# Ten rows of unused matmuls behind the last batch of a four-layer graph attention kernel

## The chip, the cores and the metric

The kernel runs on one core of one Trainium2 chip. The metric is the device time of an execution in microseconds (us), from many engines working side by side: PE (TensorE, with its weight loads counted apart as PEld), DVE (VectorE), ACT (ScalarE), POOL (GpSimd) and SP (SyncE, which issues most DMAs). The time before is 2933.31 us, the median of two runs (2930.95 and 2935.68 us).

## The reference

32 graphs of 512 nodes with 256 features each go through four attention layers, all in fp32. What is computed for one layer, cut to its core:

```python
h = jnp.maximum(_layernorm(x), 0.0)
Wh = h @ W
e = leaky_relu(Wh @ a1 [:, :, None] + Wh @ a2 [:, None, :], alpha)
e = jnp.where(adj, e, -inf)
x = x + act(softmax(e) @ Wh)      # elu, relu, elu with 4 heads
```

The fourth layer is an MLP (256 to 512), an attention without a mask over 512 features, a second MLP (512 to 256) and an attention with the mask; then relu, and the sum with x. The result is x after the fourth layer.

## The kernel before, in words

The function `fast` keeps the weights, the adjacency (`maskT`, bf16, 128 partitions by 4 by 512) and the identity in SBUF for the whole run. Its logits are exponentials of sums, so that a masked weight tile is one DVE instruction (L353, max and multiply with `maskT`). One batch is a generator that yields between pieces of work. Four such streams run at a time (`NS` is 4), each working through every fourth batch, and the loop at the end of `fast` always advances the stream whose due time is the earliest. [...] The last batch, number 31, has nothing beside it at its end: its pieces at L676 to L720 follow one another, with one row tile per step (`n = 1`).

Nearly all matmuls are fp32 and are issued at L66 (`matmul`) and L70 (`transpose`). In the trace an fp32 matmul leaves two records on PE, each with a weight load of its own on PEld, and a transpose leaves one. A matmul writes to a bank of PSUM (128 partitions by 512 fp32), handed out by `bank()` at L76 to L80: four names with two buffers each, used in turn when no other stream is active, so that a bank comes back after eight allocations.

Behind the loop, L789 to L799 make a single number, `flag`: the DVE reduces what `note` (L306) has collected in `seen` to `bad` (128 by 1), PE transposes `bad` to one row (L797), and the DVE reduces this to `one` (L798) and compares (L799). All engines then load `flag` (L1203) and branch on it (L1204). In this run it is zero, and the engines jump over the second version of the kernel, `general`, to the end of the program.

Of the kernel before, what the change touches and what calls it, by code (L numbers as in the profile page):

```python
# [19 lines left out]
FP = mybir.dt.float32  # L20
# [4 lines left out]
OP = mybir.AluOpType  # L25
AX = mybir.AxisListType

EPS = 1.0e-5
P = 128
# [6 lines left out]
def fast(ctx, tc, flag, x, adj, w0, a0, w1, a1, w2, a2, mlp1_w, mlp1_b, mlp2_w, mlp2_b,  # L36
         w_fc, a_fc, w_hand, a_hand, out):
    nc = tc.nc
# [13 lines left out]
    work = ctx.enter_context(tc.tile_pool(name="work", bufs=2))  # L52
# [24 lines left out]
    def bank():  # L77

        own = [turn[0], *(i for i in range(NS) if i not in active and i != turn[0])]
        banks[0] += 1  # L80
        return psum.tile([P, N], FP, tag=f"b{own[banks[0] % len(own)]}", name="b", bufs=8 // NS)
# [3 lines left out]
    ident = const.tile([P, P], FP, name="ident")  # L85
# [78 lines left out]
    for h in range(NH):  # L164
        t, r = divmod(h * D, P)
# [6 lines left out]
    WM1 = const.tile([P, KF, H], FP, name="WM1")  # L172
# [24 lines left out]
    maskT = const.tile([P, NT, N], BF, name="maskT")  # L197
# [572 lines left out]
    while ready:  # L770
        i = min(ready, key=ready.get)
# [14 lines left out]
            ready[i] = wait  # L786


    worst = const.tile([P, 3], FP, name="worst")  # L789
    nc.vector.tensor_reduce(worst[:, 0:1], seen, AX.X, OP.max)  # L790
    nc.vector.tensor_scalar(worst[:, 0:1], worst[:, 0:1], LIMIT, None, op0=OP.is_gt)
# [3 lines left out]
    p = bank()  # L795
    transpose(p[:1, :P], bad, ident)
    one = const.tile([1, 1], FP, name="one")  # L797
    nc.vector.tensor_reduce(one, p[:1, :P], AX.X, OP.max)  # L798
    nc.vector.tensor_scalar(flag, one, 0.5, None, op0=OP.is_gt)  # L799


@with_exitstack
# [394 lines left out]
@with_exitstack  # L1197
def kernel(ctx: ExitStack, tc: tile.TileContext, *args):
    nc = tc.nc
    keep = ctx.enter_context(tc.tile_pool(name="keep", bufs=1))  # L1200
    flag = keep.tile([1, 1], I32, name="flag")
    fast(tc, flag, *args)
    bad = nc.values_load(flag[0:1, 0:1], min_val=0, max_val=1)  # L1203
    with tc.If(bad > 0):  # L1204
        general(tc, *args)
# [27 lines left out]
```

## Time and profile before

| what | us |
|---|---|
| median of two runs | 2933.31 |
| span of the profiled execution, first to last instruction | 2929.6 |
| PE busy in the span | 2858.9 (98%) |
| DVE busy | 2219.9 (76%) |
| ACT busy | 1536.8 (52%) |
| last matmul for the result (transpose of `rT`) starts | 2920.99 |
| transpose of `bad` starts | 2921.10 |
| `flag` is written | 2922.26 |
| last counted instruction (sum into x, L715) ends | 2925.34 |
| mean TensorE clock granted, as a share of full speed | 0.996 |

The profiled execution is the only one with a trace. Its span leaves out what an execution does before the first and after the last instruction; the median of the runs is 3.7 us above it. Engines in a trace have a row each, and a row shows when an instruction was busy and what it waited for. Register, branch, semaphore and load-to-register instructions are not counted as busy: they are in the trace's records, but in none of the groups. So between 2925.34 us and the end at 2929.64 us the groups show nothing, though the program is still at work: the last DMAs of the output land, and the engines load the flag, branch and meet at a barrier.

### The profile page before, as it was taken

The numbers are of one execution on the slowest core, as the hardware profiler recorded it, in microseconds if no ns is written. First come the engines' busy times: TensorE is split into PE (matmuls) and PEld (weight loads), VectorE is DVE, ScalarE is ACT, GpSimd is POOL, SyncE is SP. The second block draws the span as 40 slices with busy tenths as digits, with TensorE's granted clock in tenths as the row PEclk, the third lists the DMA queues.
The fourth block names the chain that finished last, engine by engine and source line by source line (L and its number), as shares of the span: only waits on it lengthen the run. The fifth ranks groups of instructions, "written<-read, shape, count | busy, mean of one in ns | idle before, by whom it ended". The sixth has DMA issues, their size and how long they took to land.

```text
span 2929.6 us, 43083 instructions
## 1 busy us (share of the span) xinstructions
PE 2858.9 (98%) x15177; PEld 2329.5 (80%) x15177; DVE 2219.9 (76%) x5676; ACT 1536.8 (52%) x3922; POOL 502.3 (17%) x515
## 2 busy tenths in 40 slices
PE   8999999999999999999999999999999999999998
PEld 6777887877888877888877888788887788877876
DVE  4677877778778778778778777787787787777764
ACT  4444455555555555555554556545555555555444
POOL 0011112112122111122021121111221111211220
PEclk9999999999999999999999999999999999999999
DMA  3033223233223333233332233222332322323230
GB/s 94 19 102 102 80 88 116 91 98 95 88 94 106 93 100 98 84 102 96 100 102 80 89 115 93 91 97 91 94 116 80 102 93 88 104 93 96 90 107 30
DMA packets 193182, 270.89 MB, mean 92 GB/s; under 512 B 17024, under 2 KB 156094, under 8 KB 192960
## 3 DMA queue, kind: packets, MB, share of 16 engines
q1 hardware_dynamic: 163200, 169.76, 18.5%
q0 software_dynamic: 29760, 98.30, 10.4%
q8 instruction: 123, 2.02, 0.3%
q14 instruction: 99, 0.81, 0.1%
HBM read 152.62 MB, written 115.39 MB: 91 GB/s over the span
## 4 chain that ended last, share of the span: by engine, by line
PE 82%; DVE 10%; ACT 4%; DMA 3%; issue 1%; SPq 0%; POOL 0%; DVEq 0%; POOLq 0%; ACTq 0%
PE b L66 75%; PE b L70 7%; DVE st L269 2%; DMA g<-table,at 2%; DVE sums L641 1%; DVE xn L280 1%; DVE x L406 1%; DVE y L405 1%; ACT v L325 1%; DVE sums L632 1%; ACT y L505 1%; ACT q L504 1%; DVE w L353 1%; ACT hT L290 1%; DVE tot L646 0%
## 5 line engine op out<-in xcount | busy, mean ns | idle before, releaser
L66 PE MATMUL b<-v,w 128*128 128x65 f32 (+1 forms) x7232 | 1218.0, 321 | 10.6 <-DVE w L353 10.5
L66 PEld LDWEIGHTS b<-v,w 128*128 128x128 f32 x7232 | 1050.0, 191 | 168.7 <-issue 56.1
L66 PE MATMUL b<-WFC,oT 128*128 128x256 f32 (+1 forms) x2048 | 495.2, 380 | 0.0
L66 PEld LDWEIGHTS b<-WFC,oT 128*128 128x128 f32 x2048 | 374.5, 189 | 49.3
L66 PE MATMUL b<-W,hT 128*128 128x259 f32 (+1 forms) x1536 | 388.8, 391 | 22.8 <-DVE v L463 14.1
L353 DVE SCALAR_TENSOR_TENSOR w<-b,v,maskT 128x512 f32<-128x512 f32 x512 | 369.4, 744 | 5.1 <-PE b L70 4.1
L607 POOL DMA_INDIRECT order<-v,at x248 | 277.0, 1117 | 490.7 <-DVE oT L730 152.3
L66 PEld LDWEIGHTS b<-W,hT 128*128 128x128 f32 x1536 | 285.3, 192 | 75.3 <-DVE v L463 17.1
L715 POOL TENSOR_TENSOR x<-x,y 128x512 f32<-128x512 f32 x62 | 87.8, 1416 | 1063.7 <-ACT y L713 950.0
L353 DVE SCALAR_TENSOR_TENSOR w<-spread,v,maskT 128x512 f32<-128x512 f32 x384 | 269.5, 742 | 0.0
L66 PE MATMUL b<-hT,WM 128*128 128x512 f32 x512 | 250.0, 599 | 0.7 <-ACT hT L290 0.7
L66 PE MATMUL b<-oT,WM 128*128 128x512 f32 x512 | 231.2, 594 | 0.0
L655 POOL DMA_INDIRECT g<-table,at x124 | 120.9, 975 | 642.8 <-ACT y L675 292.0
L387 DVE RECIPROCAL rden<-b 128x1 f32<-128x1 f32 (+1 forms) x516 | 77.3, 162 | 184.8 <-PE b L66 183.0
L529 ACT ACTIVATE v<-b,ends 128x256 f32<-128x256 f32 x256 | 118.8, 467 | 177.2 <-PE b L66 172.9
L269 DVE BATCH_NORM_STATS2 st<-x 128x6 f32<-128x256 f32 x512 | 193.3, 409 | 6.4 <-DMA x<-in_x_dram 4.1
L412 DVE TENSOR_TENSOR y<-q,y 128x512 f32<-128x512 f32 (+1 forms) x194 | 132.9, 685 | 82.9 <-ACT q L411 45.0
L339 ACT ACTIVATE oT<-b,bias 128x512 f32<-128x512 f32 x128 | 87.7, 686 | 182.7 <-PE b L66 182.0
L290 ACT ACTIVATE hT<-b 128x512 f32<-128x512 f32 x256 | 146.5, 592 | 70.3 <-PE b L70 70.2
L66 PEld LDWEIGHTS b<-oT,WM 128*128 128x128 f32 x512 | 97.5, 191 | 95.7 <-issue 92.4
L70 PE MATMUL b<-ident,xn 128*128 128x128 f32 x1024 | 147.4, 275 | 6.7 <-DVE xn L280 4.0
L70 PEld LDWEIGHTS b<-ident,xn 128*128 128x128 f32 x1024 | 123.7, 143 | 31.9 <-DVE xn L280 5.2
(143 smaller groups left out, 3748.1 us busy)
## 6 DMA issues: line engine op xcount, KB each, us to landing
table<-sums SPq DMA_DIRECT2D x62, 1032.0 KB
sums<-order SPq DMA_DIRECT2D x62, 516.0 KB
spread<-row SPq DMA_DIRECT2D x96, 256.0 KB
x<-in_x_dram SPq DMA_DIRECT2D x32, 512.0 KB
out_dram<-x SPq DMA_DIRECT2D x62, 256.0 KB
sums<-order SPq DMA_DIRECT2D x62, 129.0 KB
order<-v,at POOLq DMA_INDIRECT x248
g<-table,at POOLq DMA_INDIRECT x124
```

Of the source, the lines that this page charges most:

```text
L66: nc.tensor.matmul(p, w, x, **flags)
L70: instruction = nc.tensor.transpose(p, x, i)
L269: nc.vector.bn_stats(st[:, i, :], xt[:, t0 + i, :])
L290: nc.scalar.activation(hT[:, :, t0 * P:(t0 + 2) * P], p.rearrange("p (k n) -> p k n", k=KF), AF.Relu)
L339: nc.scalar.activation(o[:, f, :], p, AF.Relu, bias=bias[:, f:f + 1])
L353: w = nc.vector.scalar_tensor_tensor(wt[:, j, :], r, t_col(j), maskT[:, j, :], op0=OP.max, op1=OP.mult)
L387: nc.vector.reciprocal(r, den)
L412: nc.vector.tensor_tensor(r, q, r, op=OP.add)
L529: nc.scalar.activation(halves[c][:, t, :F], ps[:, :F], AF.Copy, scale=ends[:, t, 0:1])
L607: nc.gpsimd.indirect_dma_start(out=orders[c], out_offset=bass.IndirectOffsetOnAxis(ap=at[:, 0, t:t + 1], axis=0), in_=halves[c][:, t, :], ...
L655: nc.gpsimd.indirect_dma_start(out=g, out_offset=None, in_=table, in_offset=bass.IndirectOffsetOnAxis(ap=at[:, 1, t:t + 1], axis=0),)
L715: (nc.gpsimd if n == 2 else nc.vector).tensor_tensor(xr, xr, y, op=OP.add)
```

## The change

A function `rows` is called once, behind the loop over the streams and ahead of the reduction of `seen`. It copies 128 by 512 of the weights `WM1` to a tile `half` of type fp32r (DVE), copies the identity to a tile of fp32r that nothing reads, and then issues ten rows of matmuls, each matmul with `start` and `stop` set. A row goes to one bank (the tenth to two), and when it is done a DVE reduction over 64 columns writes one number to `got`, which nothing reads. `keep_in_program_order` ties the matmuls of a row to the order in which they are written. In `tile_position=(r, c)` r is the first row of the array that the matmul uses and c the first column.

```diff
+    rows(nc, tc, work, bank, ident, maskT, WM1)
+
     worst = const.tile([P, 3], FP, name="worst")
...
+FR = mybir.dt.float32r
...
+def rows(nc, tc, work, bank, ident, maskT, WM1):
+    near = WM1[:, 0, :]
+    half = work.tile([P, 512], FR, tag="spread", name="half", bufs=2)
+    nc.vector.tensor_copy(half, near)
+    tile_r = work.tile([P, P], FR, tag="junk", name="tile_r", bufs=1)
+    nc.vector.tensor_copy(tile_r, ident)
+    got = work.tile([P, 16], FP, tag="tot", name="got", bufs=1)
+    sets = []
+
+    def row(count, one):
+        p = bank()
+        for i in range(count):
+            tc.keep_in_program_order(one(p, i))
+        sets.append(p)
+        c = len(sets) - 1
+        nc.vector.tensor_reduce(got[:1, c:c + 1], p[:1, :64], AX.X, OP.max)
+
+    def mm(p, w, x, **at):
+        return nc.tensor.matmul(p, w, x, start=True, stop=True, **at)
+
+    def w_of(t, i):
+        return t[:, i % 4 * P:(i % 4 + 1) * P]
+
+    row(24, lambda p, i: mm(p[:, :65], w_of(maskT[:, 0, :], i), maskT[:, 1, :65]))
+    row(12, lambda p, i: mm(p[:, :195], w_of(maskT[:, 0, :], i), maskT[:, 1, :195]))
+    row(24, lambda p, i: mm(p[:, :66], w_of(half, i), half[:, :66]))
+    row(12, lambda p, i: mm(p[:, :256], w_of(half, i), half[:, :256]))
+    row(12, lambda p, i: mm(p[:, :128], w_of(near, i), near[:, :128]))
+    row(4, lambda p, i: mm(p[:64, :], near[:, i * 64:(i + 1) * 64], near, tile_position=(0, 0)))
+    row(16, lambda p, i: mm(
+        p[i % 2 * 64:i % 2 * 64 + 64, :], near[:, i % 8 * 64:(i % 8 + 1) * 64], near, tile_position=(0, i % 2 * 64)
+    ))
+    row(16, lambda p, i: mm(
+        p[i % 4 * 32:i % 4 * 32 + 32, :], near[:, i * 32:(i + 1) * 32], near, tile_position=(0, i % 4 * 32)
+    ))
+    row(16, lambda p, i: mm(
+        p[i % 4 * 32:i % 4 * 32 + 1, :], near[:, i * 32:i * 32 + 1], near, tile_position=(0, i % 4 * 32)
+    ))
+    q = [bank(), bank()]
+    for i in range(16):
+        r = i % 2 * 64
+        tc.keep_in_program_order(mm(
+            q[i % 2][:, :65], near[r:r + 64, i % 4 * P:(i % 4 + 1) * P], near[r:r + 64, :65],
+            tile_position=(r, 0),
+        ))
+    for i in range(2):
+        nc.vector.tensor_reduce(got[:, 14 + i:15 + i], q[i][:, :64], AX.X, OP.max)
```

In the built program PE's list has the rows behind the last transposes of `rT` for the result and ahead of the transpose of `bad`. The two copies stand on the DVE in layer 2 of the last batch, between weight tiles of its last head (L353), the reductions of rows 1 and 2 among the last elementwise work of the result, and the others behind it. The lists of ACT, POOL and SP keep their work in its order, but for the load of `flag`, which on SP now stands behind the last output DMA and not between two of them.

## The prediction

> **What bounds the kernel now.** I read the page first, for which engine sets the pace, then the groups kept apart by form, for the price of a matmul, then the timeline and the chain of waits over the last 25 us, because the change stands there alone. The page:
>
> ```profile
> PE 2858.9 (98%) x15177; PEld 2329.5 (80%) x15177; DVE 2219.9 (76%) x5676; ACT 1536.8 (52%) x3922; POOL 502.3 (17%) x515
> ```
>
> PE is full for the whole span, and no other engine is. Work added to PE is paid in full unless it falls where PE is idle. The table of windows (PE, PEld, DVE, ACT and POOL busy, granted clock, DMA share, GB/s) shows the one such place:
>
> ```profile
> 2900.00:2921.00 21.00, 20.71 (x87) 14.69 (x86) 8.35 (x24) 10.41 (x25) 2.53 (x2) 1.00 0.08 26
> 2921.00:2929.60 8.60, 0.37 (x4) 0.08 (x2) 3.68 (x12) 3.25 (x9) 0.00 (x0) 0.76 0.21 70
> ```
>
> PE is done at 2921.4 us, and 8.2 us follow without it. The timeline says where PE's list ends, and what a matmul costs there:
>
> ```profile
> 2816.99 3.68 PE L66 MATMUL b<-v,w 128*128 128x65 f32 x32
> 2904.94 3.60 PE L66 MATMUL b<-oT,WM 128*128 128x512 f32 x8
> ...
> 2920.88 0.38 PE L70 MATMUL b<-ident,rT 128*128 128x128 f32 x2
> 2921.10 0.27 PE L70 MATMUL b<-ident,bad 128*1 128x128 f32 x1
> ```
>
> Start to start is a line's length less one record, over the others: (3.60 - 0.59) / 7 = 0.429 us for 512 columns, (3.68 - 0.275) / 31 = 0.110 us for 65; the single records of the second lie 0.1117 us apart, which I use. One fp32 matmul is two records. 0.429 us is 0.84 ns per column, 65 columns would stream in 0.055 us, so 0.112 us must be the load of the 128 columns of weights. The chain of waits ends with
>
> ```profile
> 2924.47 0.43 ACT y L713
> 2924.90 0.02 issue
> 2924.92 0.42 DVE x L715
> ```
>
> that is, with the last elementwise work of the result; the output DMA issued behind it, the branch and the barrier fill the 4.3 us to 2929.64.
>
> [...]
>
> **The change part by part.** Nothing is removed. PE executes in order and the rows stand between the last `rT` transposes and `bad`, so they start at 2921.1, where `bad` started. Row 1 takes the bank of the first average, eight allocations back, which ACT left at 2917.8; later rows find theirs read by 2924 to 2926, while they come at 2927 and later, so I charge no wait for banks.
>
> 1. 24 bf16, 65 columns: half of the fp32 load, 0.060 us: 1.4 us. Bounds 0.030 (streaming 27 ns and a little) and 0.112 [...]: 0.7 to 2.7.
> 2. 12 bf16, 195 columns: half of an fp32 record's 0.84 ns per column, [...] 195 x 0.42 = 82 ns and 2 of overhead: 0.084 us, 1.0 together (1.3 if the load is 0.112).
> 3. 24 fp32r, 66 columns. [...] As one record with the load of an fp32 record: 24 x 0.112 = 2.7 us. Bounds: 1.4 as bf16, 5.4 as full fp32.
> 4. 12 fp32r, 256 columns: in one pass 256 x 0.42 ns and 2 are 0.109 us: 1.3 us; as fp32 the row of `WFC,oT` gives two records 0.216 us apart: 5.2. I take 1.3.
> 5. 12 fp32, 128 columns: 24 records x 0.112 = 2.7 us.
> 6. 4 fp32, 512 columns, one column group: 8 x 0.429 = 3.4 us.
> 7. to 9. Each 16 fp32 matmuls, 512 columns, in two, four and four column groups. Without overlap 32 x 0.429 = 13.7 us each, 41.2 together. With free overlap 6.9 + 3.4 + 3.4 = 13.7. I take a value between: the two records of a matmul use the same group, so the second waits for the first; in program order the next matmul's first record can only run beside this one's second. That is one record time per matmul however many groups there are: 17 x 0.429 = 7.3 us each, 21.9 together.
> 10. 16 fp32, 65 columns, two row groups: the load of 128 columns binds, 32 x 0.112 = 3.6 us; 1.8 if two loads go side by side.
>
> Four changes of mode (into row 6, between 7 and 8, into and out of 10) at the part of a record that normally overlaps, 0.592 - 0.429 = 0.16 us: 0.7 us. Sum S = 1.4 + 1.0 + 2.7 + 1.3 + 2.7 + 3.4 + 21.9 + 3.6 + 0.7 = 38.7 us.
>
> Behind the rows `flag` becomes the last thing in the program. The final matmul drains 0.16; the two reductions over 128 partitions take 0.2 each (0.195 for `seen` 128x48), `one` 0.27, `flag` 0.14, with about 0.06 of hand-over. In the trace's uncounted records, PE loads the flag 0.04 us after it is written (2922.26), is at its branch at 2923.06 and only goes on at 2926.92: 4.66 us from flag to PE past the branch. This was hidden under the last output; now it is on the path. From the last engine past its branch (DVE, 2928.555) to the end took 1.09. So the end is 2921.1 + S + 0.16 + 0.4 + 0.27 + 0.14 + 0.06 + 4.66 + 1.09 = 2966.6, that is S - 1.8 = +36.9 us on 2929.6. The median of the runs stood 3.7 above the span and I leave that: 2933.3 + 36.9 = 2970.2.
>
> The rest I cost at nothing. The copies (0.43 for 128x512, from `W<-raw` at L231, and some 0.2) push the last weight tile of head 3 from 2809.8 to 2810.4; PE reads it at 2816.99, and the DVE idles 3.19 us at 2810.5. Without that cover they would cost 0.6. The reductions of rows 1 and 2 wait for PE at 2922.7 and 2923.7, and L412, L712 and L715 of the result are queued behind them: the last sum into x comes some 0.9 us later, its DMA with it, all under the rows, which run to 2959. SP's later flag load is behind its last DMA, and waits for the flag anyway.
>
> **Rivals.**
> A, my forecast, pairs overlap: +36.9. With the bounds of rows 1 to 4 and 10, 2966 to 2978.
> B, the column groups of fp32 do not overlap at all: S grows by 41.2 - 21.9 = 19.3, +56.2, 2989.6. For: nothing before shows any overlap. [...] This is the case on the other side of 2%: the limit is 58.7 us, so it decides as soon as rows 1 to 4 cost 2.5 us more than I took; with fp32r at the fp32 price (+6.6) it gives 2996.
> C, full packing: S falls by 8.2, +28.7, 2962; with the low ends of rows 1, 3 and 10, 2958. [...]
> D, the clock: the last window was granted 0.76, when PE sat idle. Should partly used columns count as idle and the clock fall to half, S doubles: +75.6, 3009. Against: the table has 1.00 where PE is busy.
> E, the unused rows are dropped, or PE takes them in earlier gaps: 2933, no slower. PE's list holds them all at the end, and PE had no gap of that size; almost excluded.
>
> **How the numbers follow.** A 0.45, B 0.26 (0.09 of it over 2%), C 0.22, D 0.04, E 0.03. About 2% is what a measurement of this kernel tells from no change. Slower by over 2%: 0.09 + 0.04 = 0.13. Faster by over 2% needs an accident: 0.01. The rest, 0.86, is within 2%, though A, B and C are all real additions. The range runs from the low end of C, 2958, to B with part of its upper bound, 2993; outside are E, the lower tip of C, D and the dear half of B, about 0.18. A's own range is 2965 to 2979.
>
> **What would show it.** Rows 7, 8 and 9 last 7.3 us each (A), 13.7 (B), or 6.9, 3.4 and 3.4 (C). Row 6 is 3.4 and row 5 2.7, or the fp32 price is wrong. One record per fp32r matmul, 0.11 us apart in rows 3 and 4. PE's first new matmul at 2921.1, `flag` about 0.9 us after PE's last row, the end 5.8 after that. The granted clock stays at 1.00. It is wrong if the groups behave unlike each other, if the branch is served faster from a flag that comes late, or if fp32r costs like fp32.

## The result, and the profile after

The changed kernel took 2965.9 us, the median of two runs (2965.75 and 2966.06), against 2933.31: a ratio of 1.0111, 95% interval 1.0092 to 1.0131. That is within 2%, inside the range, and 4.3 us below the forecast. A repetition further down puts the ratio at 1.0095, and the traces show what stretched the profiled execution of this first comparison. The page of the changed kernel says

```profile
PE 2893.4 (98%) x15409; PEld 2350.2 (79%) x15409; DVE 2223.4 (75%) x5689; ACT 1536.9 (52%) x3922; POOL 505.4 (17%) x515
```

PE is 34.5 us busier, and its weight loads 20.7. Of the 34.5 us, the rows are 28.0; where the others come from is asked further down. The windows (PE, PEld, DVE, ACT and POOL busy, granted clock, DMA share, GB/s), cut at the start of the rows and at their end, place it:

```profile
2900.00:2929.20 29.20, 28.91 (x130) 21.71 (x129) 13.24 (x34) 15.13 (x35) 2.54 (x2) 1.00 0.06 19
2929.20:2957.60 28.40, 28.37 (x236) 15.97 (x234) 5.20 (x21) 3.24 (x9) 0.00 (x0) 1.00 0.06 20
2957.60:2964.30 6.70, 0.00 (x0) 0.00 (x0) 0.48 (x4) 0.00 (x0) 0.00 (x0) 0.59 0.04 10
```

The rows fill 28.0 us without a gap at a full clock, and 6.7 us of flag, branch and barrier follow. The chain of waits now ends with PE, not with the sum into x:

```profile
2929.44 27.98 PE b L826 x232
2957.42 0.34 DVE got L854 x2
2957.76 0.20 DVE one L800
2957.95 0.02 issue
2957.98 0.14 DVE flag L801
```

The groups kept apart by form (busy us, mean ns of one record) give the rows' share. Row 6 and row 7 have one form, 40 records:

```profile
L826 PE MATMUL b<-WM 128*64 128x512 f32 x40 | 10.5, 595 | 0.0
L826 PE MATMUL b<-WM 128*32 128x512 f32 x32 | 3.6, 595 | 0.0
L826 PE MATMUL b<-WM 128*1 128x512 f32 x32 | 3.6, 592 | 0.0
...
L826 PE MATMUL b<-WM 64*128 64x65 f32 x32 | 2.0, 275 | 0.0
...
L826 PE MATMUL b<-maskT 128*128 128x65 bf16 x24 | 0.9, 193 | 0.0
```

32 records of 512 columns in 3.6 us: if one record of few columns of weights takes 0.429 us like a full one, they ran four at a time. (That it does is shown below, with all of them in one column group.) The weight loads show it too. A line of the timeline is a burst, and from row 7 to row 9 the bursts hold more:

```profile
2940.12 0.14 PEld L826 LDWEIGHTS b<-WM 128*64 128x64 f32 x1 [0.29 <-issue]
2940.55 0.19 PEld L826 LDWEIGHTS b<-WM 128*64 128x64 f32 x3 [0.29 <-issue]
...
2949.25 0.13 PEld L826 LDWEIGHTS b<-WM 128*32 128x32 f32 x4 [0.30 <-issue]
2949.68 0.13 PEld L826 LDWEIGHTS b<-WM 128*32 128x32 f32 x4 [0.30 <-issue]
```

In row 8 four loads come every 0.43 us, the spacing of the records of one group, so each burst feeds four groups. Row by row, from one row's first record to the next row's (rows 6 and 7 overlap in the trace; the cut between them is at 2941.40 us, where the column group that both use takes its first record of row 7):

| row | forecast us | trace us |
|---|---|---|
| 1, bf16, 65 columns | 1.4 | 0.73 |
| 2, bf16, 195 | 1.0 | 0.95 |
| 3, fp32r, 66 | 2.7 | 2.68 |
| 4, fp32r, 256 | 1.3 | 1.50 |
| 5, fp32, 128 | 2.7 | 2.77 |
| 6, one column group | 3.4 | 3.48 |
| 7, two groups | 7.3 | 6.96 |
| 8, four groups | 7.3 | 3.46 |
| 9, four groups, one column each | 7.3 | 3.55 |
| 10, two row groups | 3.6 | 1.93 |
| changes of mode | 0.7 | in the rows |
| sum | 38.7 | 28.0 |

**Where the other 8 us are.** The rows are 28.0 us, and the end comes 7.0 us after the start of `bad` where it came 8.5 after it before: +26.5 us. The profiled execution was 34.7 us longer. The rest, 8.2 us, lies ahead of the rows: they start at 2929.3, not at 2921.1, though PE's list up to there is the same. It was lost in steps of 0.5 to 2 us, each in a few us. One of them, the same 12 records in before and then in the changed kernel, by the timeline:

```profile
1538.98 2.95 PE L66 MATMUL b<-W,hT 128*128 128x268 f32 x12 [1.82 <-DVE v L463]
```

```profile
1541.88 4.64 PE L66 MATMUL b<-W,hT 128*128 128x268 f32 x12 [1.87 <-DVE v L463]
```

The idle time ahead is alike (1.82 and 1.87 us), but the records take 4.64 us instead of 2.95. The windows around them give the clock, before first:

```profile
1539.00:1543.00 4.00, 4.00 (x18) 3.46 (x19) 1.52 (x4) 1.19 (x4) 0.00 (x0) 1.00 0.00 0
```

```profile
1542.00:1546.00 4.00, 4.00 (x11) 3.11 (x12) 0.71 (x2) 0.79 (x3) 0.00 (x0) 0.57 0.00 0
```

The trace's record of the granted clock has a stretch of 3.41 us at half speed here. Between the start and the last work for the result there were eight in this execution, six of 3.41 us and two of 6.83, 34.1 us together, and four in that of before, three of 3.41 and one of 10.24, 20.5 us together. What became of PE up to that point, before first:

```profile
0.00:2921.00 2921.00, 2858.48 (x15176) 2329.46 (x15177) 2216.25 (x5664) 1533.52 (x3914) 502.32 (x515) 1.00 0.29 93
0.00:2929.20 2929.20, 2865.07 (x15176) 2334.21 (x15177) 2217.75 (x5666) 1533.63 (x3914) 505.39 (x515) 0.99 0.29 92
```

The same 15176 records kept PE busy for 6.6 us longer, and for another 1.6 us it was idle.

### The profile page after: what moved, and what is told of

It reads as the page before. It is cut to its first block, busy times and chain, and to the rows that moved or that the text cites. A ratio compares the mean times of both kernels' runs of the same rounds, so it can differ in the third digit from the quotient of the medians.

```text
span 2964.3 us, 43564 instructions
## 1 busy us (share of the span) xinstructions
PE 2893.4 (98%) x15409; PEld 2350.2 (79%) x15409; DVE 2223.4 (75%) x5689; ACT 1536.9 (52%) x3922; POOL 505.4 (17%) x515
## 4 chain that ended last, share of the span: by engine, by line
PE 79%; DVE 11%; ACT 4%; DMA 4%; issue 2%; SPq 0%; POOL 0%; POOLq 0%; DVEq 0%; ACTq 0%
PE b L66 71%; PE b L70 7%; DVE st L269 2%; DMA g<-table,at 2%; DMA order<-v,at 1%; DVE xn L280 1%; PE b L826 1%; DVE sums L641 1%; DVE x L406 1%; DVE y L405 1%; ACT v L325 1%; DVE w L353 1%; DVE sums L632 1%; ACT y L505 1%; DMA sums<-order 1%
## 5 line engine op out<-in xcount | busy, mean ns | idle before, releaser
L353 DVE SCALAR_TENSOR_TENSOR w<-b,v,maskT 128x512 f32<-128x512 f32 x512 | 369.5, 745 | 5.1 <-PE b L70 3.9
L353 DVE SCALAR_TENSOR_TENSOR w<-spread,v,maskT 128x512 f32<-128x512 f32 x384 | 269.6, 742 | 0.0
```

The lines of the kernel that those rows point to most:

```text
L353: w = nc.vector.scalar_tensor_tensor(wt[:, j, :], r, t_col(j), maskT[:, j, :], op0=OP.max, op1=OP.mult)
```

## The experiments

Each changes the changed kernel unless said otherwise. No row's result is used in any of them; three (other orders, four records, prices) put other rows in the place of the ten. These three were executed once each, and what is said of them is read from their traces, not from their times.

### All in one column group

```diff
-        p[i % 4 * 32:i % 4 * 32 + 32, :], near[:, i * 32:(i + 1) * 32], near, tile_position=(0, i % 4 * 32)
+        p[:32, :], near[:, i * 32:(i + 1) * 32], near, tile_position=(0, 0)
```

and likewise in rows 7 and 9.

> Rows 7, 8 and 9 keep their matmuls, but every one of them uses column group 0, so nothing can run beside anything. If the groups are what made rows 8 and 9 short in the trace (8 clusters of four records, 0.429 us apart), each of the three rows now lasts 32 x 0.429 = 13.7 us, the rows grow from 14.3 to 41.2 us and the median by 27 us, to 2993 us. The rival: a record with few columns of weights is cheap by itself (32 columns or 1); then rows 8 and 9 stay near 3.4 us, only row 7 grows, and the median rises by about 6 us.

2988.0 us, ratio 1.0189 (1.0172 to 1.0205). The groups by form:

```profile
L826 PE MATMUL b<-WM 128*64 128x512 f32 x40 | 17.4, 593 | 0.0
L826 PE MATMUL b<-WM 128*32 128x512 f32 x32 | 13.9, 593 | 0.0
L826 PE MATMUL b<-WM 128*1 128x512 f32 x32 | 13.9, 593 | 0.0
```

Rows 8 and 9 take 13.9 us each, 3.9 times as long, with 0.429 us from one record to the next in all three rows, and all rows take 55.5 us in place of 28.0. The median stands 27 us above that of the repetition further down (2960.8 us), as expected; the 2993 us were counted from the first 2965.9. The rival is out: a record with one column of weights took what one with 64 took (0.429 us), and the packing is what made rows 8 and 9 short (3.5 us each in place of 13.9). This is also what my rival B would have been.

### The groups in blocks

```diff
-        p[i % 4 * 32:i % 4 * 32 + 32, :], near[:, i * 32:(i + 1) * 32], near, tile_position=(0, i % 4 * 32)
+        p[i // 4 * 32:i // 4 * 32 + 32, :], near[:, i * 32:(i + 1) * 32], near, tile_position=(0, i // 4 * 32)
```

and likewise in rows 7, 9 and 10.

> The same matmuls as in the changed kernel, but with all matmuls of one group ahead of those of the next: rows 7 (8 + 8), 8 and 9 (4 + 4 + 4 + 4) and 10 (8 + 8). If PE starts matmuls in program order and a busy group holds up all behind it (the rule on which my 7.3 us per row stood), only the records at a border overlap: row 7 takes 31 x 0.429 = 13.3 us, rows 8 and 9 take 29 x 0.429 = 12.4 us each, row 10 takes 31 x 0.112 = 3.5 us, and the median rises by some 26 us to 2992. If each group takes its matmuls from what is waiting, whatever stands ahead of them, the rows stay as long as they are (6.9, 3.4, 3.4 and 1.8 us) and the median stays at 2966. Anything between says how far ahead PE looks.

2976.7 us, ratio 1.0159 (1.0142 to 1.0176): neither. Row 7 took 12.2 us, row 8 8.7 us and row 10 3.3 us. The bursts of weight loads show where the next group came in, in row 8:

```profile
2944.75 0.14 PEld L826 LDWEIGHTS b<-WM 128*32 128x32 f32 x2 [0.81 <-issue]
...
2946.06 0.11 PEld L826 LDWEIGHTS b<-WM 128*32 128x32 f32 x1 [0.32 <-issue]
2946.49 0.14 PEld L826 LDWEIGHTS b<-WM 128*32 128x32 f32 x3 [0.32 <-issue]
...
2948.24 0.14 PEld L826 LDWEIGHTS b<-WM 128*32 128x32 f32 x3 [0.32 <-issue]
```

A burst of three is the start of a group. They are 1.75 us apart, about four records of 0.429 us: the next group started with the fifth of the eight records of the one before, when three had not started. In rows 7 and 10, with 16 records to a group, it was with the thirteenth: 28 records one behind another are 12.0 us at 0.429 us and 3.1 at 0.112, against 12.2 and 3.3 measured. I took this for a rule that PE passes over at most three records.

### Other orders

Four rows of 16 in place of the ten: fp32 with two matmuls in turn for each of four column groups, then bf16 with one in turn, with four in turn, and all in one group.

```diff
...
+    bf, mov = maskT[:, 0, :], maskT[:, 1, :]
     row(16, lambda p, i: mm(
-        p[i % 4 * 32:i % 4 * 32 + 32, :], near[:, i * 32:(i + 1) * 32], near, tile_position=(0, i % 4 * 32)
+        p[i // 2 % 4 * 32:i // 2 % 4 * 32 + 32, :], near[:, i * 32:(i + 1) * 32], near,
+        tile_position=(0, i // 2 % 4 * 32)
     ))
+    row(16, lambda p, i: mm(
+        p[i % 4 * 32:i % 4 * 32 + 32, :], bf[:, i * 32:(i + 1) * 32], mov, tile_position=(0, i % 4 * 32)
+    ))
+    row(16, lambda p, i: mm(
+        p[i // 4 * 32:i // 4 * 32 + 32, :], bf[:, i * 32:(i + 1) * 32], mov, tile_position=(0, i // 4 * 32)
+    ))
+    row(16, lambda p, i: mm(p[:32, :], bf[:, i * 32:(i + 1) * 32], mov, tile_position=(0, 0)))
```

> Other rows in place of the ten, all of 16 matmuls with 32 columns of weights and 512 moving columns: fp32 with two matmuls in turn for each of four groups; bf16 with one in turn; bf16 with four in turn; bf16 all in one group. From the kernel with blocked order, PE passes over three records that wait for their group, not more. By this rule the fp32 row takes 4.8 us, against 6.0 if it passes two, 4.3 if four and 3.5 if there is no limit. A bf16 matmul should be one record of 0.216 us: 0.9 us in turn, 1.5 us with four in turn by the rule of three (1.7 with two, 1.3 with four, 2.8 if nothing is passed), and 3.5 us in one group.

The rule fell. The fp32 row with two matmuls in turn took 3.5 us, not 4.8, and the bf16 row with four in turn 0.9 us, not 1.5; bf16 in one group took 3.5 us. The bursts of the fp32 row:

```profile
2922.79 0.18 PEld L826 LDWEIGHTS b<-WM 128*32 128x32 f32 x8 [0.17 <-ACT y L713]
2923.25 0.15 PEld L826 LDWEIGHTS b<-WM 128*32 128x32 f32 x4 [0.28 <-issue]
```

Eight weight loads come within 0.18 us at its start, and 3.5 us is about the time of eight records of 0.429 us, as many as one group has: the four groups ran side by side from the start, and the fourth passed nine waiting records. What fits the times of all rows up to here is that a group held up the next one only while more than four of its records were not done. Here every turn is four records, in the blocks it was eight or 16.

### Four records per group

Three rows in place of the ten: four groups in bf16 with six and with five matmuls each, and in fp32 with three (six records) each.

```diff
...
+    bf, mov = maskT[:, 0, :], maskT[:, 1, :]
+    def run(count, turn, w, x):
+        row(count, lambda p, i: mm(
+            p[i // turn * 32:i // turn * 32 + 32, :], w[:, i % 16 * 32:(i % 16 + 1) * 32], x,
+            tile_position=(0, i // turn * 32)
+        ))
+    run(24, 6, bf, mov)
+    run(20, 5, bf, mov)
+    run(12, 3, near, near)
```

> Other rows in place of the ten, 32 columns of weights and 512 moving columns: 24 bf16 with six in turn for each of four groups, 20 bf16 with five in turn, 12 fp32 with three in turn (six records). The kernel with other orders contradicted the rule that PE passes three records: there nine were passed. What fits all rows so far: PE hands records out in program order, each column or row group keeps four of them (one running, three waiting), and only a fifth for a full group holds up the rest. By this rule the rows take 2.6, 1.8 and 5.2 us, with the groups 0.43, 0.22 and 0.86 us apart. With room for three per group it would be 3.3, 2.4 and 6.5; for five 2.0, 1.3 and 3.9; with no limit 1.3, 1.1 and 2.6.

The three rows took 2.65, 1.9 and 5.2 us. The first records of the groups came 0.448, 0.448 and 0.447 us apart in the row with six in turn, 0.23 us with five, and 0.89 us in the fp32 row, where the bursts of weight loads give it:

```profile
2934.76 0.14 PEld L826 LDWEIGHTS b<-WM 128*32 128x32 f32 x3 [0.32 <-issue]
2935.18 0.14 PEld L826 LDWEIGHTS b<-WM 128*32 128x32 f32 x2 [0.29 <-issue]
2935.61 0.17 PEld L826 LDWEIGHTS b<-WM 128*32 128x32 f32 x4 [0.29 <-issue]
...
2936.50 0.17 PEld L826 LDWEIGHTS b<-WM 128*32 128x32 f32 x4 [0.29 <-issue]
```

A new group joins at 2934.76, 2935.65 and 2936.54, the second and third within the bursts of four. The three rows are as long as forecast with four records to a group (2.6, 1.8 and 5.2 us); the forecasts with three or five are off by half a us to 1.3 us in each row.

### Everything twice

```diff
-    rows(nc, tc, work, bank, ident, maskT, WM1)
+    for _ in range(2):
+        rows(nc, tc, work, bank, ident, maskT, WM1)
```

> All that the change adds is there twice, copies included. By the trace the rows take 28.0 us from the first to the transpose of bad; all else of the difference of the two profiled executions (34.7 us) lies ahead of the rows (8.2 us) or at the end. If only PE's own time for the rows counts, the second set adds 28 us to the changed kernel: median 2994. If the rows or the copies also slow the work ahead of them, the second set adds what the first did, 32.6 us: 2998.5.

2992.4 us, ratio 1.0199 (1.0182 to 1.0217). In the trace the first set takes 28.03 us and the second 28.03 too. The medians alone can't tell 28 from 32.6: against the repetition below the second set adds 1.04% with some 0.25% of uncertainty, 23 to 38 us.

### The copies alone

The rows and the reductions to `got` are left out, the two copies to fp32r tiles stay. Everything behind them in `rows` goes, from

```diff
-    got = work.tile([P, 16], FP, tag="tot", name="got", bufs=1)
-    sets = []
```

on.

> Only the two copies to fp32r tiles are left; no row, no reduction to got. The 8.2 us that the changed kernel's profiled execution lost ahead of its rows went with seven stretches of 3.4 us at half TensorE clock that the profile of before has not at the same places. If these come and go from execution to execution, this kernel takes 2933 us, as before, with a scatter of some us, and in its profile the time at which PE finishes goes with the number of such stretches, 1.7 us each. If the copies or the changed lists cause the loss, it takes 2937 to 2941 us.

2934.9 us, ratio 1.0007 (0.9997 to 1.0018): no cost that can be told from none, though up to 5 us are not excluded.

### The changed kernel again, and a control

First the changed kernel without an edit, more often.

> The changed kernel once more, against before in the same rounds, because the result stands on two runs each and before alone has since ranged from 2925 to 2940 us. By the traces the rows take 28.0 us between the last transpose of rT and bad, and the end comes 7.0 us after bad, not 8.5: +26.5 us over before if nothing ahead of the rows is changed, about 2959. The rival is that the copies or the changed lists also cost time ahead of the rows, as the 32.6 us of the first comparison would have it: 2965.

2960.8 us (five runs) against 2933.0 (27 runs), ratio 1.0095 (1.0079 to 1.0111): 27.9 us, with the 26.5 of the trace inside 23.2 to 32.6. The 32.6 us of the first comparison lie at the upper end of this, so some of them were probably chance.

Then the kernel before without an edit.

> The kernel before, unchanged, timed as if it were an experiment: 2932 us, a ratio of 1.000, with runs between 2925 and 2940. It shows how far the ratio of the kernel with the copies alone (1.0007) can come from chance. In its profile PE's last transpose of rT should come later the more stretches of half clock there are: 2921 us with 20 us of them, half of each further us on top.

2933.1 us (22 runs), ratio 1.000 (0.9992 to 1.0008). The runs of before alone ranged from 2925 to 2943 us over all sessions. The profiles show a part of the reason. In each, the us at half clock ahead of the last work for the result, and the time at which PE went on to its next record:

| profile | us at half clock | PE through at |
|---|---|---|
| groups in blocks | 17.1 | 2920.4 |
| before | 20.5 | 2921.1 |
| control | 23.9 | 2922.8 |
| prices | 23.9 | 2922.4 |
| copies alone | 23.9 | 2926.6 |
| other orders | 27.3 | 2922.8 |
| changed, again | 27.3 | 2924.0 |
| twice | 27.3 | 2927.1 |
| one group | 34.1 | 2927.5 |
| changed | 34.1 | 2929.3 |
| four records | 41.0 | 2931.0 |

A straight line through them gains 0.46 us per us at half clock and leaves 1.5 us of scatter; the copies alone, which I had expected on it, lie 3.1 us above. PE's busy time up to that point keeps closer to a line: from 2857.5 us (groups in blocks) to 2867.8 us (four records) it gains 0.43 us per us at half clock, with 0.4 us of scatter. What is left is PE's idle time, 61 to 66 us: 65.9 with the copies alone, and 61.3 to 64.7 in the kernels that have the copies and rows, so the copies don't explain it.

So nearly half of the time at half clock is lost. The 13.6 us by which the changed kernel's first profile exceeds that of before account for 6.3 of the 8.2 us by the line. The rows are not the cause: kernels with rows stand at both ends of the table. Why a stretch comes in one execution and not in the next was not tested.

### Prices by type and width

Six rows in place of the ten, each of one type and width.

```diff
...
+    bf, mov = maskT[:, 0, :], maskT[:, 1, :]
+    row(24, lambda p, i: mm(p[:, :65], w_of(bf, i), mov[:, :65]))
+    row(24, lambda p, i: mm(p[:127, :65], w_of(bf, i)[:, :127], mov[:, :65]))
+    row(24, lambda p, i: mm(p[:64, :65], bf[:, i % 8 * 64:(i % 8 + 1) * 64], mov[:, :65], tile_position=(0, 0)))
+    row(12, lambda p, i: mm(p, w_of(bf, i), mov))
+    row(24, lambda p, i: mm(p[:, :128], w_of(half, i), half[:, :128]))
+    row(12, lambda p, i: mm(p, w_of(half, i), half))
```

> Rows for prices in place of the ten. 24 bf16 with 65 moving columns, with 128, 127 and 64 columns of weights: row 1 showed 30 ns for 128. [...] 12 bf16 of 512 columns: 0.216 us. fp32r with 128 columns (24): bound by the load, 0.112 us; with 512 (12): one pass, 0.216 us, half of the fp32 record and a quarter of an fp32 matmul.

Start to start: bf16 with 65 moving columns 0.030 us at 128 columns of weights, 0.059 at 127 and 0.033 at 64; bf16 of 512 columns 0.216; fp32r of 128 columns 0.112 and of 512 columns 0.227. The loads themselves (mean ns of one):

```profile
L826 PEld LDWEIGHTS <-maskT 128*128 128x128 bf16 x36 | 2.0, 98 | 1.2
L826 PEld LDWEIGHTS <-maskT 128*127 128x127 bf16 x24 | 1.5, 140 | 0.0
```

With one column less a load took 140 ns in place of 98, and the row twice as long (0.059 us a matmul in place of 0.030). An fp32r matmul left one record: with 128 moving columns at the spacing of one fp32 record (0.112 us), with 512 at about half of that spacing (0.227 against 0.429 us).

### A use of the rows in the kernel before

The kernel before (without any rows), with weights and values of layers 0 and 1 and of the last attention as fp32r, so that these aggregations are computed in fp32r, on 258 columns in place of 257.

```diff
-        v = work.tile([P, NT, F + 3], FP, tag="v", name="v", bufs=4)
+        v = work.tile([P, NT, F + 3], FR, tag="v", name="v", bufs=4)
...
-        wt = work.tile([P, NT, N], FP, tag="w", name="w", bufs=4)
+        wt = work.tile([P, NT, N], kind, tag="w", name="w", bufs=4)
...
-        aggregate(p[:, :F + 1], wt, t, lambda j: v[:, j, :F + 1])
+        aggregate(p[:, :F + 2], wt, t, lambda j: v[:, j, :F + 2])
```

> Not a part of the change but of the kernel before: the aggregations of layers 0 and 1 and of the last attention take their weights and values as fp32r tiles (258 moving columns in place of 257), written so by DVE and ACT; all else stays fp32. The rows showed one record for an fp32r matmul where fp32 has two at the same spacing. 1536 matmuls would then save one record each, 0.22 us, 338 us of PE's 2859. If PE still sets the pace the median falls to about 2600 us; if the DVE (2220 us busy) or the order of the streams takes over, somewhere between 2600 and 2800. The rival: fp32r gains nothing where weights change with each matmul: 2933.

2661.6 us, ratio 0.9068 (0.9051 to 0.9086), faster than both kernels. By form, before had 3104 records of 128x257 in 756.0 us, of which 32 remain elsewhere as fp32, and now there are 1536:

```profile
L67 PE MATMUL b<-v,w 128*128 128x258 f32 x1536 | 390.5, 363 | 15.2 <-ACT y L425 10.2 <-DVE w L355 3.1
```

PE's busy time falls by 324 us, to 2534.8, close to the 338 forecast, and the median by 272. By the pages of the two profiled executions, whose spans differ by 254.9 us, PE is busy for 324.1 us less and idle for 69.2 us more (139.9 in place of 70.7), the longest of it before `hT` of ACT (25.6 us) and before weight tiles of the DVE (`w`, 19.3 us). So of the 338 us, 14 are missing in the busy time and 69 went into idle time. The granted clock was lower too, 0.957 on average in place of 0.996, with 235 us at half clock in place of 27; how much of the 14 and of the 69 us goes back to that was not tried. Nor was it measured how the results differ from those in fp32.

## Why the prediction was right, point by point

The number came out right, and the mechanism behind its largest term was wrong.

- **The place.** Right: PE was full, the rows started where `bad` had stood (at 2929.28 us, 0.11 behind the start of the last transpose of `rT`, with `bad` behind them at 2957.30), none waited for its bank, and they were paid in full. Twice the rows took twice 28.03 us.
- **Rows 2 to 6.** Right to 0.2 us each: an fp32 record of 512 columns every 0.429 us, one of 128 columns every 0.112 us, one record for fp32r. The 0.2 us of row 4 are records 0.118 us apart in place of 0.109, and 0.20 us behind the first one; the cause of both stays open.
- **Rows 7 to 9.** The step that failed: "in program order the next matmul's first record can only run beside this one's second". That was an assumption, and across groups the order did not hold: the first record for the second group of row 7 started at 2940.55, before the last record of row 6 at 2940.97, which stands ahead of it. (The trace does not name the group. But of the 40 records of rows 6 and 7, 24 follow one another at 0.429 us from the start of row 6, as many as the first group has, and the other 16 do so from 2940.55.) The second record of a matmul did come behind the first, by 0.43 to 0.45 us in row 8, but the records of four groups started within 0.02 us of one another each time. Row 7 came out at about my figure (6.96 us for 7.3) because its two groups side by side took half of the 13.7 us of one; rows 8 and 9 were 3.46 and 3.55 us, as in rival C. Against one column group, four gave 13.9 / 3.5, about 4.
- **Row 10.** My lower bound, 1.8, was right (1.93 us) and the value 3.6 wrong: the records started in pairs, 0.007 us apart, with 0.112 us from one pair to the next. The same holds for row 1, at the lower bound again: 0.030 us a matmul. Its weight loads took 97 ns each, half of the 192 ns of fp32, but the matmuls did not come at half of the fp32 spacing. My 0.060 us was an estimate, and is what 127 columns took (0.059); no bf16 row of 65 moving columns came near my upper bound of 0.112 us.
- **The changes of mode.** About 0.09 us each, not 0.16: into row 6 the records are 0.205 us apart in place of 0.112, between rows 7 and 8 and into row 10 0.523 in place of 0.429, and out of row 10 0.201 in place of 0.112.
- **The end.** I had S - 1.8; the traces give S - 1.5. PE was past its branch 4.53 us after the flag (4.66 forecast), but it was not the last: POOL's drain behind the branch, 4.49 us long in both traces, ended 0.8 us later still.
- **The sum.** With S = 28.0 my own formula gives +26.3 us, and the repetition measured 27.9 (23.2 to 32.6). The forecast of +36.9 was 10.7 us too much in S, 7.9 of it in rows 7 to 9. That the first comparison came within 4.3 us of it was luck: the profiled execution lost 8.2 us ahead of the rows, which I had not forecast, and these hid most of the 10.7. The mechanism of A was wrong. C was right, with low ends for rows 1 and 10: by its terms 2959.5 us, against 2960.8 in the repetition.
- **Rival D.** Wrong: 1.00 throughout the rows, one column of weights included. Half clock came behind the rows (0.59 over 6.7 us) and ahead of them (34.1 us), not in them.

## What to carry to other kernels

Before costing small matmuls, ask how many groups of the array they can take in turn: with at most four records in a row to a group (two fp32 matmuls, four in bf16), all four groups ran side by side here (16 matmuls in 3.5 and 0.9 us), and the order of writing decided it: in blocks the fp32 row took 8.7 us. For bf16 matmuls of 65 moving columns, use the full 128 columns of weights rather than one less (0.030 us each against 0.059). Where PE sets the pace and the accuracy allows it, look at fp32r: it took 272 us off the kernel before. Read a difference of less than a few tenths of a per cent only with many runs, or from the traces.

## What the runs showed of the hardware that was not expected

- A group's first record waited while the group ahead of it in the list had more than four records left: 1.75 us between groups with eight fp32 records each, 0.89 with six, 0.447 with six in bf16, 0.23 with five. With four no such wait shows: 3.5 us for the whole row in fp32, 0.9 in bf16.
- 127 columns of bf16 weights cost 0.059 us where 128 cost 0.030 and 64 cost 0.033.
- An fp32r matmul is one record where an fp32 matmul is two: 0.227 us for 512 columns, against 2 x 0.429.
- Stretches at half clock of 3.41, 6.83 and 10.24 us in the traces of before and of the changed kernel, and 17 to 41 us of half clock ahead of the rows in executions of the same work, with 0.43 us more busy time of PE for each us. One stretch followed 1.87 us of idle PE in the changed kernel, where 1.82 us at the same place in the kernel before had none behind them.
- A narrow record is not cheaper: one column of weights and 512 moving columns took 0.429 us a record, like 32, 64 or 128 columns.
